# First attention of a two-layer kernel: the inner loop in half steps of two tiles instead of single tiles

## The chip, the cores and the metric

The kernel runs on one core of a Trainium2 chip. The metric is the device time of one execution in microseconds (us); lower is better. The engines are TensorE (PE, matrix products; PEld are its loads of weights), VectorE (DVE), ScalarE (ACT), GpSimd (POOL) and SyncE (SP, whose queue starts DMA transfers). Products land in PSUM, which has eight banks of 128 x 512 floats, and are read from there by VectorE or ScalarE.

## The reference

One sequence of 2048 tokens with 128 channels passes four stages. Each adds its result to x, and each works on a layer norm of x:

```python
x = x + L0_attn(layernorm(x))   # 16 heads of 64, low-rank q, k, v, rotary
x = x + L0_ffn(layernorm(x))    # 16 experts, 4 chosen per token in 2 of 4 groups
x = x + L1_attn(layernorm(x))   # 8 heads; 96 keys per query, chosen by an index score
x = x + L1_ffn(layernorm(x))    # shared expert and 2 of 8 experts by hash
```

The change is in the first stage. Its core, for each head, is

```python
scores = einsum('bhqd,bhkd->bhqk', q, k) * scale
attn = softmax(scores, axis=-1)          # over all 2048 keys
out = einsum('bhqk,bhkd->bhqd', attn, v)
out = out.reshape(b, s, H * DH) @ w_out.T + residual
```

All data are 32-bit floats.

## The kernel before, in words

The first attention has 32 units: eight pairs of heads times four groups of 512 queries, all pairs of a group before the next group. A unit has 16 tiles. The scores are computed twice, once with queries on the partitions and once with keys on the partitions.

*By query* (`by_query`, L313): for one tile of 128 queries and 512 keys, two products "pa" (L323), one for each head of the pair. Each uses 64 rows of TensorE's array, so that both run side by side (the form "64*128" in the profile's rows). VectorE then copies each, negated, into a tile "neg" and takes the smallest value of each row, which gives the largest score (L329). `sums` (L331) lets ScalarE take the exponential of the copy and add it up by row (L340). `close`, `inverse` and `turn` make of these the maximum and the sum of each query over all keys, and the row "mrow" with the maxima.

*By key* (`by_key`, L377): for one tile of 128 keys and 512 queries, two products "pb" (L384) of the same form, and two small bf16 products (L386) that subtract the maxima ("mrow"). ScalarE takes the exponential into a tile "e" (L390).

*Weighted block* (`mean`, L392): two products "po" (L399) that add the e-weighted latent values into one PSUM bank. They use 128 rows and 64 columns of the array each (form "128*64"). After the last tile of a unit, ScalarE copies the bank into "o" (L404), and `project` (L408) multiplies by the output weights and adds to x.

`rope` (L283) makes the rotated queries of the next unit and, for the first eight units, the rotated keys (L299, L302 on VectorE, the sum L303 on POOL); keys go out to DRAM and come back in pieces "ka" and "kb" by SP's queue, whose order is written by hand. Products of pa, pb and rope take turns in five PSUM banks (pool "ps"); "po" has one bank, and all other products share two (pool "px"). The tiles "e" and the two intermediate tiles of a rope share seven buffers.

`run` (L422) writes all this as steps of four tiles. By key runs five steps behind by query, and the weighted blocks one step behind by key. When the eight units of a group are done, the following three stages of that group (`follow`: `experts0`, `attention1`, `experts1`) are woven in: they are a generator, and `advance(us)` lets it issue as many of its pieces as the given time pays for. In `attention1`, `choose` (L820) searches the largest index scores on VectorE, `gather` fetches the chosen rows by DMAs that POOL issues, `queries` and `attend` do the rest; `rotate` (L92) is used for keys, queries and gathered keys. The stages of the fourth group run alone at the end.

Within an engine, instructions run in the order of the compiled program. A scheduler makes that order from the order of issue, from priorities (copies, sums and exponentials have a high one) and from its own estimate of when operands are ready.

Of the kernel before, what the change touches and what calls it, by code (L numbers as in the profile page):

```python
# [8 lines left out]
F32 = mybir.dt.float32  # L9
# [8 lines left out]
P = 128  # L18
T = 2048
NT = T // P  # L20
# [15 lines left out]

CHOSEN = [((11 * r) % NE1, (11 * r + 7919) % NE1) for r in range(8)]
NA = 2 * NT + 1
LATE = 1
URGENT = 500  # L40
PACE = (1.0, 1.1, 1.2, 1.2)

# [1 line left out]
def bcast(ap, axis, n):  # L44

    shape = list(ap.shape)
    return ap.unsqueeze(axis).to_broadcast(shape[:axis] + [n] + shape[axis:])
# [43 lines left out]

def rotate(nc, eng, pool, out1, out2, mu, cos, sin, tag, bufs=None, keep=None):  # L92

    shape = list(mu.shape)
    c = pool.tile(shape, F32, tag=tag + "c", name=tag + "c", bufs=bufs)
    s = pool.tile(shape, F32, tag=tag + "s", name=tag + "s", bufs=bufs)
    first = eng.tensor_tensor(c, mu, bcast(cos, 2, 2), ALU.mult)
    if keep is not None:
        keep(first)
    second = eng.tensor_tensor(s, mu, bcast(sin, 2, 2), ALU.mult)  # L100
    if keep is not None:
        keep(second)
    eng.tensor_tensor(out1, c[:, :, 0, :], s[:, :, 1, :], ALU.subtract)
    eng.tensor_tensor(out2, s[:, :, 0, :], c[:, :, 1, :], ALU.add)


class Program:
# [205 lines left out]
    def by_query(self, u, i):  # L313


        nc = self.nc
        kc, qt = divmod(i, 4)
        if i == 0:
            self.ms[u] = [self.am.tile([P, 4, 4, 2], F32, tag=f"mx{k}", name=f"mx{k}_{u}") for k in range(2)]
        q, k = self.qs[self.UNITS[u]], self.kcs[(u, kc, "a")]  # L320
        ps = [self.bank(f"pa{u}_{i}_{h}") for h in range(2)]
        for h, rows in enumerate(self.HALVES):
            nc.tensor.matmul(ps[h], q[rows, qt * P : qt * P + P], k[rows, :], start=True, stop=True)  # L323
        mx = self.ms[u][0]
        with self.tc.high_priority(URGENT):
            for h in range(2):
                at = (slice(None), qt, kc, slice(h, h + 1))
                t = self.negs[(u, i, h)] = self.am.tile([P, 512], F32, tag="neg", name=f"neg{u}_{i}_{h}", bufs=5)
                nc.vector.tensor_scalar(t, ps[h], -1.0, None, ALU.mult, ALU.min, accum_out=mx[at])  # L329

    def sums(self, u, i):  # L331
# [90 lines left out]
    def run(self):  # L422

        self.prologue()
        NU = len(self.UNITS)
        BEHIND = 5
        for c in range(2):  # L430
            self.keys_of(0, c, "a")
        stream, owed, pace = self.early, 0.0, 0.8

        def advance(us):
            nonlocal stream, owed
            if stream is None:
                return
            owed += us * pace
            while owed > 0 and stream is not None:
                cost = next(stream, None)  # L440
                if cost is None:
                    stream = None
                else:
                    owed -= cost


        with self.tc.manual_schedule(engines={mybir.EngineType.SP}):
            for s in range(4 * NU + BEHIND + 5):
                u, j = divmod(s, 4)
                ub, jb = divmod(s - BEHIND, 4)  # L450
                um, jm = divmod(s - BEHIND - 1, 4)
                if u < NU and j == 0 and u + 1 < NU:
                    self.rope(self.UNITS[u + 1][0], "q", self.UNITS[u + 1][1])
                if u + 1 < 8:
                    self.rope(u + 1, "k", j)
                if s == 4 * 8 - 4:
                    for _ in stream or ():
                        pass
                    stream, owed = None, 0.0
                    self.late.close()  # L460
                if s == 4 * 8:
                    self.keys.close()
                if s + 2 < 4 * NU:
                    self.keys_of((s + 2) // 4, (s + 2) % 4, "a")
                sb = s + 2 - BEHIND
                if 0 <= sb < 4 * NU:
                    self.keys_of(sb // 4, sb % 4, "b")
                for i in range(4):
                    if 0 <= ub < NU:
                        self.by_key(ub, 4 * jb + i)  # L470
                    advance(1.0)
                    if u < NU:
                        self.by_query(u, 4 * j + i)
                    advance(1.0)
                    n = 4 * s + i
                    if 0 <= n - LATE < 16 * NU:
                        self.sums(*divmod(n - LATE, 16))
                    if i == 3 and u < NU and j == 3:
                        self.close(u)
                    if i == 2 and j == 0 and 0 <= u - 1 < NU:  # L480
                        self.turn(u - 1)
                        self.inverse(u - 1)
                    if 0 <= um < NU:
                        self.mean(um, 4 * jm + i)
                    advance(1.0)
                    if i % 2 == 1 and jm == 1 and 0 <= um - 1 < NU:
                        self.project(um - 1, i // 2)
                if jm == 1 and 0 <= um - 1 < NU:
                    self.outs.pop(um - 1)
                    if um % 8 == 0:  # L490
                        if stream is not None:
                            for _ in stream:
                                pass
                        stream, owed = None, 0.0
                        if um < NU:
                            stream, pace = self.follow(um // 8 - 1), PACE[um // 8 - 1]

        self.first.close()
        self.alone = True
        for _ in self.follow(3):  # L500
            pass
# [219 lines left out]
    def attention1(self, sc, g):  # L721
# [4 lines left out]
        xr, cs, kT, kiT, table = self.xr[g], self.cs, self.kT, self.kiT, self.table  # L726
# [7 lines left out]
        with ExitStack() as prep:  # L734
# [17 lines left out]
            for i, (dst, wt) in enumerate(  # L752
# [5 lines left out]
                o, s = dst, pm[:m, :]  # L758
                if i in (1, 2):
                    o = o.rearrange("p (n a g) -> p n a g", a=4, g=32)  # L760
                    s = s.rearrange("p (n g a) -> p n a g", a=4, g=32)
# [17 lines left out]
        sm = sc.enter_context(tc.tile_pool(name="c_sm", bufs=2, side="right"))  # L779
# [8 lines left out]
        def index_scores(n):  # L788

            width = 64 + 128 * n  # L790
            q = slice(P * (n % 4), P * (n % 4) + P)
            v = sm.tile([P, T - 64], F32, tag="v", name=f"v{n}", bufs=2 if self.alone else 1)
            for lo in range(0, width, 512):
                hi = min(lo + 512, width)
                for h in range(4):
                    rows = slice(64 * (h % 2), 64 * (h % 2) + 64)
                    pi = self.x(f"pi{n}_{lo}_{h}", [P, 512])
                    nc.tensor.matmul(pi[:, : hi - lo], qiT[h // 2][rows, q], kiT[rows, lo:hi], start=True, stop=True)  # L798
                    if h == 0:
                        nc.vector.tensor_scalar(v[:, lo:hi], pi[:, : hi - lo], 0.0, w["iw"][:, 0:1], ALU.max, ALU.mult)  # L800
                    else:
                        rl = sm.tile([P, 512], F32, tag="rl", name=f"rl{n}_{lo}_{h}", bufs=6 if self.alone else 2)
                        nc.scalar.activation(rl[:, : hi - lo], pi[:, : hi - lo], AF.Relu)  # L803
                        nc.vector.scalar_tensor_tensor(  # L804
                            v[:, lo:hi], rl[:, : hi - lo], w["iw"][:, h : h + 1], v[:, lo:hi], ALU.mult, ALU.add
                        )
                    if h % 2 == 1:
                        yield pay(2.0)


            vmask = w["vmask"]
            if n == 0:
                nc.vector.tensor_tensor(v[:, 0:64], v[:, 0:64], vmask[:, 1, 0:64], ALU.min)
                nc.vector.tensor_copy(v[:, 64:128], vmask[:, 1, 64:128])
                width = P
            else:
                nc.vector.tensor_tensor(v[:, width - P : width], v[:, width - P : width], vmask[:, 0, :], ALU.min)
            vs[n] = v[:, 0:width]
# [83 lines left out]
        def attend(n):  # L902
            (kv, cl), (qs, ql) = chosen.pop(n), qTs.pop(n)

            for i in range(2):
                half = kv[:, 16 * i : 16 * i + 16, 32:64]

                rotate(
                    nc, nc.vector, sm, half[:, :, 0:16], half[:, :, 16:32],
                    half.rearrange("p r (a b) -> p r a b", a=2),  # L910
                    bcast(cs[:, 0, 2 * NT, :], 1, 16), bcast(cs[:, 1, 2 * NT, :], 1, 16), "rg", 1,
                    tc.keep_in_program_order,
                )
                yield pay(2.0)
# [317 lines left out]
```

## Time and profile before

| what | value |
|---|---|
| time, median of 5 runs | 3233.21 us |
| lowest and highest of the 5 | 3225.97 and 3250.67 us |
| the profiled execution's own time | 3255.46 us |
| its span, first to last instruction | 3253.4 us |
| mean granted clock of TensorE | 0.884 |
| waits of POOL's L303 for VectorE's t_q | 1028.4 us |
| waits of VectorE's L329 for TensorE's pa | 525.0 us |
| waits of ScalarE's L340 for VectorE's neg | 443.1 us |

A row of the profile's groups reads: line, engine, operation, output from input, shapes, count, then busy time in us and mean ns of one, then the idle time of that engine just before these instructions and what ended it. A row of a timeline reads: start in us from the span's start, duration in us, engine, line, operation, names, shapes, and how many instructions are merged. One product of 32-bit floats leaves two records, one for each of its two passes through the array. The slices show the span in 40 equal parts of 81 us, each digit the busy share in tenths.

### The profile page before, as it was taken

To read this page: it belongs to the slowest core of one execution; us is meant where nothing else is said; L and a number is where in the kernel's file an instruction comes from. 1 tells how busy PE (TensorE), PEld (TensorE's weight loads), DVE (VectorE), ACT (ScalarE), POOL (GpSimd) and SP (SyncE) were. 2 spreads that over 40 slices of the span, in tenths; PEclk is the share of its full clock that TensorE was granted. 3 is DMA by queue.
4 is the path that set the end of the run, shared out by engine and by line. 5 is a ranking of instruction groups with operands and counts; after the bars stand their busy time and mean duration, and the time that the engine had idled before them with its cause. 6 is when DMAs were issued, how large, how long until landed. Compare 5 with 4: busy or idle time off the path is not lost. (4 is left out here: it accounts for less than half of the span.)

```text
span 3253.4 us, 39029 instructions
## 1 busy us (share of the span) xinstructions
PE 2732.4 (84%) x13452; PEld 1136.1 (35%) x13452; DVE 1682.8 (52%) x4650; ACT 1801.0 (55%) x4190; POOL 580.9 (18%) x586
## 2 busy tenths in 40 slices
PE   6999999998798899997798889999789769773436
PEld 3333333343243344332233334343233324431224
DVE  7655554655344445664445534666526343585433
ACT  4777778666475567665465557656455435331224
POOL 2111000002313210002313220001222230007330
PEclk9999999999798899998798889999889789875557
DMA  4221111111111111111111111111111010101000
GB/s 147 60 59 49 59 49 41 49 42 37 33 34 40 32 46 48 41 41 30 34 31 38 30 27 54 46 46 27 30 30 35 22 24 27 40 14 25 13 13 28
DMA packets 98100, 127.76 MB, mean 39 GB/s; under 512 B 31344, under 2 KB 49776, under 8 KB 97904
## 3 DMA queue, kind: packets, MB, share of 16 engines
q1 hardware_dynamic: 81520, 108.48, 11.5%
q0 software_dynamic: 16384, 16.81, 2.2%
q8 instruction: 106, 1.74, 0.2%
q14 instruction: 90, 0.74, 0.1%
HBM read 115.26 MB, written 9.96 MB: 38 GB/s over the span
## 5 line engine op out<-in xcount | busy, mean ns | idle before, releaser
L329 DVE TENSOR_SCALAR_CACHE_REDUCE neg<-pa 128x512 f32<-128x512 f32 x1024 | 671.3, 686 | 680.5 <-PE pa L323 525.0
L340 ACT ACTIVATE neg<-neg,mx 128x512 f32<-128x512 f32 x1024 | 734.7, 718 | 497.4 <-DVE neg L329 443.1
L390 ACT ACTIVATE e<-pb 128x512 f32<-128x512 f32 x1024 | 554.6, 593 | 332.4 <-PE pb L386 234.0
L323 PE MATMUL pa<-ka,q 64*128 64x512 f32 x2048 | 677.8, 630 | 57.7 <-DVE neg L329 36.2
L384 PE MATMUL pb<-q,kb 64*128 64x512 f32 x2048 | 670.6, 661 | 58.7 <-ACT e L390 44.4
L843 POOL DMA_INDIRECT kv<-table,ixT x512 | 493.1, 963 | 804.8 <-issue 307.0
L399 PE MATMUL po<-e,ckv 128*64 128x512 f32 x2048 | 588.0, 640 | 9.5 <-issue 6.8
L323 PEld LDWEIGHTS pa<-ka,q 64*128 64x128 f32 x2048 | 239.7, 194 | 287.5 <-issue 105.2
L384 PEld LDWEIGHTS pb<-q,kb 64*128 64x128 f32 x2048 | 194.6, 192 | 404.0 <-DVE neg L329 145.0
L303 POOL TENSOR_TENSOR q<-t_q 128x512 f32<-128x512 f32 x32 | 40.9, 1278 | 1501.1 <-DVE t_q L302 1028.4
L386 PE MATMUL pb<-mrow,onesb 64*128 64x512 bf16 x1024 | 236.8, 388 | 4.0 <-issue 4.0
L399 PEld LDWEIGHTS po<-e,ckv 128*64 128x64 f32 x2048 | 106.6, 137 | 332.3 <-issue 301.9
L340 ACT ACTIVATION_READ_ACCUMULATOR neg<-neg,mx 128x1 f32 x1024 | 193.8, 189 | 0.0
L798 PE MATMUL pi<-kiT,qiT 64*128 64x512 f32 (+4 forms) x320 | 124.3, 659 | 56.9 <-issue 21.4
L951 DVE TENSOR_REDUCE mx<-pl 128x2 f32<-128x416 f32 x64 | 37.8, 591 | 245.4 <-remote 144.5
L955 ACT ACTIVATE e<-pl,mx 128x208 f32<-128x208 f32 x128 | 54.5, 431 | 172.1 <-DVE mx L952 155.2
L804 DVE SCALAR_TENSOR_TENSOR v<-rl,iw_sb,v 128x512 f32<-128x512 f32 (+4 forms) x120 | 77.2, 649 | 80.2 <-ACT rl L803 52.4
L945 PE MATMUL pl<-kr,qT 64*32 64x128 f32 x1024 | 61.6, 302 | 62.4 <-issue 62.4
L717 DVE SCALAR_TENSOR_TENSOR hb<-thb,zb 128x512 f32<-128x512 f32 x64 | 44.3, 692 | 127.3 <-ACT zb L715 127.3
L386 PEld LDWEIGHTS <-onesb 64*128 64x128 bf16 x1024 | 63.2, 97 | 124.1 <-issue 118.4
L803 ACT ACTIVATE rl<-pi 128x512 f32<-128x512 f32 (+4 forms) x120 | 57.5, 508 | 83.5 <-PE pi L798 36.2
L894 PE MATMUL ptq<-ident,qq 128*128 128x128 f32 x256 | 51.5, 344 | 61.8 <-issue 29.5
(276 smaller groups left out, 2871.0 us busy)
## 6 DMA issues: line engine op xcount, KB each, us to landing
ka<-kd SPq DMA_DIRECT2D x128, 256.0 KB
kb<-kd SPq DMA_DIRECT2D x128, 256.0 KB
wb<-in_wx SPq DMA_DIRECT2D x64, 192.0 KB
kd<-kst SPq DMA_DIRECT2D x32, 256.0 KB
kv<-table,ixT POOLq DMA_INDIRECT x512
wd<-in_wx SPq DMA_DIRECT2D x40, 192.0 KB
csk<-in_cs SPq DMA_DIRECT2D x4, 512.0 KB
csq<-in_cs SPq DMA_DIRECT2D x4, 512.0 KB
```

Source lines behind the costliest of these rows:

```text
L323: nc.tensor.matmul(ps[h], q[rows, qt * P : qt * P + P], k[rows, :], start=True, stop=True)
L329: nc.vector.tensor_scalar(t, ps[h], -1.0, None, ALU.mult, ALU.min, accum_out=mx[at])
L340: nc.scalar.activation(t, t, AF.Exp, bias=mx[at], scale=-1.0, accum_out=su[at])
L384: nc.tensor.matmul(ps[h], k[rows, c], q[rows, :], start=True, stop=False)
L386: nc.tensor.matmul(ps[h], self.onesb[rows, :], mrow[rows, :], start=False, stop=True)
L390: nc.scalar.activation(e[:, h, :], ps[h], AF.Exp)
L399: nc.tensor.matmul(self.pos[u][cols, :], self.ckv[:, kb, :], e[:, h, :], start=(kb == 0), stop=(kb == NT - 1))
L798: nc.tensor.matmul(pi[:, : hi - lo], qiT[h // 2][rows, q], kiT[rows, lo:hi], start=True, stop=True)
L803: nc.scalar.activation(rl[:, : hi - lo], pi[:, : hi - lo], AF.Relu)
L804: nc.vector.scalar_tensor_tensor(v[:, lo:hi], rl[:, : hi - lo], w["iw"][:, h : h + 1], v[:, lo:hi], ALU.mult, ALU.add)
L843: nc.gpsimd.indirect_dma_start(out=kv[:, 2 * (g % 16) + g // 16, :], out_offset=None, in_=table[0 : P * (n + 1), :], in_offset=bass.Indire ...
L945: nc.tensor.matmul(pl[32 * j : 32 * j + 32, c, 80:NK], qs[rows, 32 * gr : 32 * gr + 32], kr[rows, gr % 16, :], start=False, stop=(c == 1),)
```

## The change

Each step of four tiles is written as two halves of two tiles: two tiles by key, the sums of two earlier tiles, two tiles by query, two weighted blocks. Before, each tile had one of each in turn. The sums on ScalarE are issued two tiles behind their copies instead of one (`LATE`), and the copies "neg" get eight buffers instead of five. The following stages are given the same total of time in a step: one after each tile by key and by query, and two after the two weighted blocks.

Two more edits make space for the buffers. `rotate` puts its two intermediate tiles into one, and for the gathered keys of `attention1` takes the two buffers of the existing tag "w4", which `queries` and `attend` use too. The index scores "v" are allocated only as wide as the group needs.

```diff
...
-LATE = 1
+LATE = 2
...
-    shape = list(mu.shape)
-    c = pool.tile(shape, F32, tag=tag + "c", name=tag + "c", bufs=bufs)
-    s = pool.tile(shape, F32, tag=tag + "s", name=tag + "s", bufs=bufs)
+    a = mu.shape[1]
+    both = pool.tile([P, 64 * a], F32, tag=tag, name=tag, bufs=bufs).rearrange("p (k a b d) -> p k a b d", k=2, a=a, b=2)
+    c, s = both[:, 0], both[:, 1]
...
-                t = self.negs[(u, i, h)] = self.am.tile([P, 512], F32, tag="neg", name=f"neg{u}_{i}_{h}", bufs=5)
+                t = self.negs[(u, i, h)] = self.am.tile([P, 512], F32, tag="neg", name=f"neg{u}_{i}_{h}", bufs=8)
...
-                for i in range(4):
-                    if 0 <= ub < NU:
-                        self.by_key(ub, 4 * jb + i)
-                    advance(1.0)
-                    if u < NU:
-                        self.by_query(u, 4 * j + i)
-                    advance(1.0)
-                    n = 4 * s + i
-                    if 0 <= n - LATE < 16 * NU:
-                        self.sums(*divmod(n - LATE, 16))
-                    if i == 3 and u < NU and j == 3:
+                for half in range(2):
+                    pair = range(2 * half, 2 * half + 2)
+                    for i in pair:
+                        if 0 <= ub < NU:
+                            self.by_key(ub, 4 * jb + i)
+                        advance(1.0)
+                    for i in pair:
+                        n = 4 * s + i - LATE
+                        if 0 <= n < 16 * NU:
+                            self.sums(*divmod(n, 16))
+                    for i in pair:
+                        if u < NU:
+                            self.by_query(u, 4 * j + i)
+                        advance(1.0)
+                    if half == 1 and u < NU and j == 3:
                         self.close(u)
-                    if i == 2 and j == 0 and 0 <= u - 1 < NU:
+                    if half == 1 and j == 0 and 0 <= u - 1 < NU:
                         self.turn(u - 1)
                         self.inverse(u - 1)
-                    if 0 <= um < NU:
-                        self.mean(um, 4 * jm + i)
-                    advance(1.0)
-                    if i % 2 == 1 and jm == 1 and 0 <= um - 1 < NU:
-                        self.project(um - 1, i // 2)
+                    for i in pair:
+                        if 0 <= um < NU:
+                            self.mean(um, 4 * jm + i)
+                    advance(2.0)
+                    if jm == 1 and 0 <= um - 1 < NU:
+                        self.project(um - 1, half)
...
-            v = sm.tile([P, T - 64], F32, tag="v", name=f"v{n}", bufs=2 if self.alone else 1)
+            v = sm.tile([P, 512 * g + 448], F32, tag="v", name=f"v{n}", bufs=2 if self.alone else 1)
...
-                    bcast(cs[:, 0, 2 * NT, :], 1, 16), bcast(cs[:, 1, 2 * NT, :], 1, 16), "rg", 1,
+                    bcast(cs[:, 0, 2 * NT, :], 1, 16), bcast(cs[:, 1, 2 * NT, :], 1, 16), "w4", None,
...
```

## The prediction

> **What bounds the kernel now.** I read the page first: which engine is full, and where in the span.
>
> ```profile
> PE 2732.4 (84%) x13452; PEld 1136.1 (35%) x13452; DVE 1682.8 (52%) x4650; ACT 1801.0 (55%) x4190; POOL 580.9 (18%) x586
> PE   6999999998798899997798889999789769773436
> PEclk9999999999798899998798889999889789875557
> ```
>
> TensorE is nearly full from slice 2 to slice 34, about 90 to 2790 us: the first attention, alone at first and later beside the stream of the following stages. The last 460 us (the follow-up of the last group) are outside the change. Then the table by stretch, in columns stretch, PE, PEld, DVE, ACT, POOL, clock, DMA:
>
> ```profile
> 100.00:600.00 500.00, 499.38 (x2297) 178.26 (x2293) 260.39 (x810) 376.03 (x878) 39.52 (x31) 1.00 0.18 51
> 1200.00:1500.00 300.00, 292.23 (x1339) 118.44 (x1337) 175.53 (x549) 192.98 (x425) 5.08 (x4) 0.99 0.16 46
> 1500.00:1900.00 400.00, 321.00 (x1644) 127.83 (x1640) 186.16 (x493) 209.38 (x513) 125.92 (x130) 0.86 0.13 33
> ```
>
> Without a stream, and beside experts0, TensorE has no gap and the full clock. Beside attention1 (third row) it is 80% busy at 0.86: other queues hold it up. The same table for pb (L384) alone gives the tiles (four records each): 141 in 100 to 600; 171 in the other full stretches (600-800, 1200-1500, 1900-2200, 2400-2500); 199 beside attention1. Last, TensorE's timeline, since a full engine gains only by shorter work:
>
> ```profile
> 205.95 1.13 PE L299 MATMUL ps_k<-ckd,wuk_sb 64*128 64x512 f32 x4
> 206.91 1.02 PE L384 MATMUL pb<-q,kb 64*128 64x512 f32 x4
> 207.77 0.38 PE L386 MATMUL pb<-mrow,onesb 64*128 64x512 bf16 x2
> 207.99 1.02 PE L323 MATMUL pa<-ka,q 64*128 64x512 f32 x4
> 208.94 1.08 PE L399 MATMUL po<-e,ckv 128*64 128x512 f32 x4
> 209.95 1.13 PE L384 MATMUL pb<-q,kb 64*128 64x512 f32 x4
> 210.91 0.38 PE L386 MATMUL pb<-mrow,onesb 64*128 64x512 bf16 x2
> ```
>
> From start to start, pb takes 0.86 us behind ps_k, which has the same form of array (64*128), but 0.96 behind po (128*64). The change of form costs 0.10. And po behind po:
>
> ```profile
> 2783.55 1.93 PE L399 MATMUL po<-e,ckv 128*64 128x512 f32 x6
> 2785.41 1.12 PE L1083 MATMUL pyd<-hd,wd 128*128 128x512 f32 x2
> ```
>
> Six records in 1.86 us, start to start, against 1.01 for four: the inner passes run at 0.43, the last takes about 0.53 and the second 0.48, as behind any change of form.
>
> **The change, part by part.** *Pairs on TensorE.* Before, two tiles are twice pb 0.96, mrow 0.22, pa 0.95, po 1.01: 6.28 us. After: pb 0.96, mrow 0.22, pb 0.86, mrow 0.22, pa 0.86 (followed by its own form), pa 0.95, po 0.91 (0.48 + 0.43), po 0.96 (0.43 + 0.53): 5.94. A pair saves 0.34 us where nothing stands inside it. The compiled order says how often that is: changes between 64*128 and 128*64 fall from 761 to 339, 422 fewer of the 512 that 256 unbroken pairs would drop. The 70 pairs of 100 to 600 stand unbroken (140), which leaves 282 of 372, or 0.76, for the rest. Priced by stretch: 70 x 0.34 = 24 us; 85 pairs in the other full stretches x 0.34 x 0.76 = 22; 100 pairs beside attention1, 26 at most. There the saving can all be waited away, or all count; I take a third, 9, since TensorE is 80% busy but in one queue with the waits. Sum 55.
>
> *Banks.* "ps" has five, taken in turn, two per pb and two per pa. In the compiled order an allocation waits for the one five before it. Who empties them, from the rows by form and the timeline:
>
> ```profile
> L340 ACT ACTIVATE neg<-neg,mx 128x512 f32<-128x512 f32 x1024 | 734.7, 718 | 497.4 <-DVE neg L329 443.1 <-issue 18.8 <-DVE kv L104 9.0
> L329 DVE TENSOR_SCALAR_CACHE_REDUCE neg<-pa 128x512 f32<-128x512 f32 x1024 | 671.3, 686 | 680.5 <-PE pa L323 525.0 <-remote 77.8 <-PE pb L386 30.7
> ```
>
> ```profile
> 1632.78 1.09 ACT L390 ACTIVATE e<-pb 128x512 f32<-128x512 f32 x2
> 1633.64 0.69 DVE L329 TENSOR_SCALAR_CACHE_REDUCE neg<-pa 128x512 f32<-128x512 f32 x1 [1.83 <-PE pa L323]
> 1634.38 0.72 ACT L340 ACTIVATE neg<-neg,mx 128x512 f32<-128x512 f32 x1 [0.51 <-DVE neg L329]
> ```
>
> Worked through for a half step with pb at 0: the first pb is complete at 1.37 (0.41 after its mrow starts, with the hand-over), ScalarE empties the four pb banks by 3.55 (4 x 0.545), VectorE the four pa banks from 3.34 to 5.89 (0.62 each from start to start), and the four sums (0.72) run from 4.08 to 7.06. The next pb completes at 5.94 + 1.37 = 7.31. So ScalarE has 0.25 us to spare, and the tightest bank, the last pa's, is empty at 3.0 for a need at 3.11. Before, the pb of a tile waited for an e with 1.2 us to spare, for VectorE with 1.3; after, it is about 0.2 and 2.1. Without a stream it just fits. The copies o and mrow (0.57 each, once per unit) cost what exceeds 0.25, some of which the next rope's 0.86 takes back: 2 us in all. Where ropes of q and k come together (eight times) four more banks are taken, and one pb waits 0.4 us: 3 us.
>
> *Sums two tiles later (LATE 2, neg from 5 buffers to 8).* In the compiled order the four sums still stand directly behind the e's of their own half step, ahead of the next e's: priority places them as soon as VectorE is done. I count nothing, gain or loss, and VectorE's wait for a neg buffer can only fall.
>
> *Work ahead of means.* mean still follows by_key by four tiles; the seven "e" tiles hold, and e_14 of each unit waits for the rope's sum on POOL (L303), as before, with the same gathers queued ahead of it. The order of SP's loads and stores and of POOL's sums and gathers is the same, entry by entry, in both compiled programs. No change.
>
> *Space.* v is cut to its need. rotate's tiles join in one, and for the gathered keys take the two "w4" tiles. In the last two blocks of the tail, VectorE's L97 then waits for TensorE's transposes of qq: it started at 3168.79 while the sixteen transposes (0.21 each from 3168.26) ran until about 3172. The two rotations behind it move by about 1.5 us, and ptr on TensorE and everything later in the block with them: 2 blocks, 3 us, between 0 (ScalarE's copies decide) and 6.
>
> Sum: -55 + 2 + 3 + 3 = -47 us on the profiled execution's 3255.5: 3208. That execution was 22 us above the median, so 3186.
>
> [...] Pairs give four banks in a row to one engine, then four to the other. [...]
>
> **Rivals.** *A: TensorE's saving counts only without a stream.* 24 - 8 = 16 us, 3217. For it: 199 tiles run at about 80%, with waits for VectorE and POOL. Against: the 171 tiles beside experts0 run at 96% or more.
>
> *B: ScalarE comes too late (slower).* The tight bank is freed by ScalarE, in whose queue the stream's copies stand. A copy of 0.59 in each of the 185 half steps beside the stream, less 0.25, is 63 us of waits. In choose, VectorE gets up to six searches between two pairs of negs where three stood (1.42 each at 1216 columns): 4.3 us more per half step, about 24 times, 0 to 103 us. Together 3249 to 3352 against the forecast's 3186; with a quarter of the searches, 3275. It decides from 47 / 185 = 0.25 us of new waiting per half step. Against it: the stream brings TensorE work as well, which gives ScalarE time.
>
> *C: the passes do not get shorter* (po behind po needs new weights for each block): 3233 + 8 = 3241. The six po in a row speak against it.
>
> **How the numbers follow.** Forecast 0.55, A 0.22, C 0.06, B 0.17. No change means within 0.5%, 16 us, about what a measurement here can tell: 3217 to 3249. The forecast is all faster; A lies on the edge (0.13 faster, 0.09 same); C is same; B is slower but for 0.01. Faster 0.68, same 0.16, slower 0.16. The range: full price for the pairs beside attention1 and no costs gives 3233 - 72 = 3161, and the wider margin for VectorE may take a little more idle time: 3150. Upward it takes in A, C and the first part of B: 3260. Outside are the rest of B (0.1) and a larger gain (0.1).
>
> **What would show it.** Timeline without a stream: pb, pb, pa, pa, po, po in 5.94 us a pair, pb behind mrow in 0.86, po behind po in 0.43 a pass. Right: 100 to 600 holds about 149 tiles in place of 141, and PE's busy time falls by 50 to 70 us. A: idle time of TensorE before pa and pb grows by as much as busy time falls. B: waits "PE pa <- ACT e" of over 40 us, or a longer attention1 stretch. Wrong altogether if the pair takes 6.28 us.

## The result, and the profile after

The changed kernel takes 3228.8 us (median of 52 runs, 3216.6 to 3239.5) against 3233.8 us of the kernel before beside it (94 runs). The ratio is 0.998, 95% interval 0.9967 to 0.9993. The forecast was 3186: of the 47 us that it expected, 5 came. In the experiments below, where all times are shorter, the same kernel came out at 1.0027 (1.0016 to 1.0038) of the kernel before.

From the page of the changed kernel's profile:

```profile
span 3235.2 us, 38832 instructions
...
PE 2706.5 (84%) x13452; PEld 1225.3 (38%) x13452; DVE 1675.6 (52%) x4650; ACT 1787.7 (55%) x4190; POOL 583.8 (18%) x586
PE   6999999998797899997698879999769787874446
PEclk9999999998797799998898889999879797985656
```

TensorE's busy time fell by 26 us, not by 50 to 70. The stretches shown before, in columns stretch, PE, PEld, DVE, ACT, POOL, clock, DMA:

```profile
100.00:600.00 500.00, 496.49 (x2353) 208.59 (x2353) 271.31 (x848) 378.94 (x907) 39.19 (x31) 1.00 0.19 54
1200.00:1500.00 300.00, 287.19 (x1330) 127.19 (x1331) 177.33 (x551) 192.76 (x423) 6.96 (x6) 0.98 0.15 44
1500.00:1900.00 400.00, 317.70 (x1632) 138.69 (x1630) 184.85 (x489) 206.99 (x510) 117.47 (x124) 0.86 0.12 32
```

Without a stream TensorE is still full (496.49 us busy of 500). From 1200 to 1500 us it now has 13 us of pauses where it had 8, at a clock of 0.98 where it had 0.99. TensorE's timeline without a stream shows the pair:

```profile
208.01 1.13 PE L384 MATMUL pb<-q,kb 64*128 64x512 f32 x4
208.97 0.38 PE L386 MATMUL pb<-mrow,onesb 64*128 64x512 bf16 x2
209.19 1.02 PE L384 MATMUL pb<-q,kb 64*128 64x512 f32 x4
210.05 0.38 PE L386 MATMUL pb<-mrow,onesb 64*128 64x512 bf16 x2
210.26 1.97 PE L323 MATMUL pa<-ka,q 64*128 64x512 f32 x8
212.16 1.94 PE L399 MATMUL po<-e,ckv 128*64 128x512 f32 x8
214.03 1.13 PE L299 MATMUL ps_k<-ckd,wuk_sb 64*128 64x512 f32 x4
```

pb 0.96, mrow 0.22, pb 0.86, mrow 0.21, pa 1.90, po 1.87: 6.02 us from start to start, for 5.94 forecast. The groups by form say what the banks do over the whole span. First pa and pb of the kernel before:

```profile
L323 PE MATMUL pa<-ka,q 64*128 64x512 f32 x2048 | 677.8, 630 | 57.7 <-DVE neg L329 36.2 <-issue 11.1 <-DVE t_q L302 6.3
L384 PE MATMUL pb<-q,kb 64*128 64x512 f32 x2048 | 670.6, 661 | 58.7 <-ACT e L390 44.4 <-issue 9.8 <-DVE neg L329 3.6
```

Then the changed kernel:

```profile
L340 ACT ACTIVATE neg<-neg,mx 128x512 f32<-128x512 f32 x1024 | 729.6, 714 | 390.0 <-DVE neg L329 362.3 <-DVE w L97 12.8 <-issue 7.2
L329 DVE TENSOR_SCALAR_CACHE_REDUCE neg<-pa 128x512 f32<-128x512 f32 x1024 | 658.6, 686 | 616.6 <-PE pa L323 444.2 <-remote 139.7 <-ACT e L390 8.4
L323 PE MATMUL pa<-ka,q 64*128 64x512 f32 x2048 | 649.8, 650 | 127.7 <-ACT e L390 71.6 <-issue 44.6 <-DVE w L97 6.1
L384 PE MATMUL pb<-q,kb 64*128 64x512 f32 x2048 | 684.3, 646 | 43.5 <-DVE neg L329 23.5 <-issue 8.3 <-DVE t_q L302 7.6
```

VectorE waits less for TensorE's pa (444.2 us where it was 525.0), and ScalarE's sums less for VectorE's neg (362.3, was 443.1). TensorE waits more: 127.7 us before pa where it was 57.7, and 71.6 of it for ScalarE's e. Before pb it waits less, 43.5 us where it was 58.7, so the two together grew by 55 us.

Where it went, read at the copies o that end each unit: the end of unit 8 moved from 618.4 to 598.1 us (20 us won), units 9 to 31 beside the stream grew from 2174.5 to 2206.9 (32 lost), and the tail behind them fell from 460.5 to 430.3. The last number did not come back: in the experiments the tail is 349 to 358 us in all kernels, 356.8 for the old order with the new space and 352.4 for the changed kernel. I take the 30 us for chance of the two executions. Without it the two profiles would give +12 us where the medians give -5, so some of the 32 will be chance too; one execution of each cannot say how much.

### The profile page after: what moved, and what is told of

It reads as the page before. It is cut to its first block, busy times and chain, and to the rows that moved or that the text cites. A ratio compares the mean times of both kernels' runs of the same rounds, so it can differ in the third digit from the quotient of the medians.

```text
span 3235.2 us, 38832 instructions
## 1 busy us (share of the span) xinstructions
PE 2706.5 (84%) x13452; PEld 1225.3 (38%) x13452; DVE 1675.6 (52%) x4650; ACT 1787.7 (55%) x4190; POOL 583.8 (18%) x586
## 5 line engine op out<-in xcount | busy, mean ns | idle before, releaser
L329 DVE TENSOR_SCALAR_CACHE_REDUCE neg<-pa 128x512 f32<-128x512 f32 x1024 | 658.6, 686 | 616.6 <-PE pa L323 444.2
L340 ACT ACTIVATE neg<-neg,mx 128x512 f32<-128x512 f32 x1024 | 729.6, 714 | 390.0 <-DVE neg L329 362.3
L323 PE MATMUL pa<-ka,q 64*128 64x512 f32 x2048 | 649.8, 650 | 127.7 <-ACT e L390 71.6
L384 PE MATMUL pb<-q,kb 64*128 64x512 f32 x2048 | 684.3, 646 | 43.5 <-DVE neg L329 23.5
L399 PE MATMUL po<-e,ckv 128*64 128x512 f32 x2048 | 538.2, 635 | 4.9 <-issue 4.9
L323 PEld LDWEIGHTS pa<-ka,q 64*128 64x128 f32 x2048 | 256.8, 197 | 361.2 <-ACT e L390 157.9
L384 PEld LDWEIGHTS pb<-q,kb 64*128 64x128 f32 x2048 | 231.6, 193 | 290.8 <-issue 142.6
L386 PE MATMUL pb<-mrow,onesb 64*128 64x512 bf16 x1024 | 263.2, 392 | 11.4 <-issue 5.8
L399 PEld LDWEIGHTS po<-e,ckv 128*64 128x64 f32 x2048 | 131.5, 142 | 321.7 <-issue 304.7
L340 ACT ACTIVATION_READ_ACCUMULATOR neg<-neg,mx 128x1 f32 x1024 | 192.0, 188 | 0.0
L386 PEld LDWEIGHTS <-onesb 64*128 64x128 bf16 x1024 | 71.2, 97 | 134.3 <-issue 124.7
L418 DVE SCALAR_TENSOR_TENSOR xr<-pp,rs,xr 128x128 f32<-128x128 f32 x256 | 72.1, 342 | 42.5 <-PE pp L415 42.5
L808 ACT ACTIVATE rl<-pi 128x512 f32<-128x512 f32 (+4 forms) x120 | 57.0, 508 | 58.7 <-PE pi L803 31.7
```

Source lines behind the costliest of these rows:

```text
L340: nc.scalar.activation(t, t, AF.Exp, bias=mx[at], scale=-1.0, accum_out=su[at])
L384: nc.tensor.matmul(ps[h], k[rows, c], q[rows, :], start=True, stop=False)
L386: nc.tensor.matmul(ps[h], self.onesb[rows, :], mrow[rows, :], start=False, stop=True)
L399: nc.tensor.matmul(self.pos[u][cols, :], self.ckv[:, kb, :], e[:, h, :], start=(kb == 0), stop=(kb == NT - 1))
L418: nc.vector.scalar_tensor_tensor(xr[:, j, :], pm[:, j, :], self.rs[u][:, j, h : h + 1], xr[:, j, :], ALU.mult, ALU.add)
```

## The experiments

Theory 1 was the forecast's own sum with rival B beside the stream: pairs save on TensorE everywhere, and there wait for ScalarE. All ratios are against the kernel before on the same chip, where it takes 2837 to 2841 us; what is known of the distance to 3234 stands at the end. The experiments ran on three chips: e1 to e4 on one, e5 to e12 on another, e13 to e16 on the third. "Stream" is the work of the following stages. "Units 9 to 31" runs from the copy o of unit 8 to that of unit 31.

**Which part of the change counts: e1, e2, e5.** e1 has the old loop and `LATE = 1` in the changed kernel; e2 has the new loop and `LATE = 2` in the kernel before; e5 is the changed kernel.

> The order of before, tile by tile with the sums one tile later, but with the changed kernel's space: rotate's joined tiles, the gathered keys' in the two w4 tiles, v cut to its need, eight neg buffers. Theory 1 (the pairs save 0.34 us each on TensorE and lose it again beside the stream, where the fifth bank of a pair waits for ScalarE; the shorter tail of the changed kernel's profile is chance): no change, 3230 to 3238 us, tail 460 us from the last copy of o. Theory 2 (the space edits shorten the tail by 20 to 30 us and the pairs alone bring nothing or lose): 3203 to 3215 us, tail 430 us.

> The half steps of two tiles and the sums two tiles later, with the space of before (rotate, v, five neg buffers). Theory 1: all of the change is in the order, so 3224 to 3234 us as the changed kernel. Theory 2: the order alone loses what the space edits hid, 3245 to 3260 us.

> The changed kernel itself, beside the kernel before on one chip with the others. Theory 1 (20 us won up to unit 8, 25 to 35 us lost in units 9 to 31, the space and the eight neg buffers nothing): 1.000 to 1.004 of the kernel before where the two stretches are as in the run of the half steps alone. Theory 2 (space edits and neg buffers shorten the tail): 0.990 to 0.995.

Measured: e1 0.9998 (0.9987 to 1.001), e2 1.0027 (1.0016 to 1.0038), e5 1.0027 (1.0016 to 1.0038). Space and buffers are worth nothing; the order of the loop is the whole effect. Up to unit 8 e5 wins 19 us over e1 (599.1 against 618.2), in units 9 to 31 it loses 29 (1889.8 against 1861.3), in the tail it wins 4. e2, on e1's chip, gives the same picture: 599.7, 1890.6 and a tail of 351.5. The table by stretch of e1, then of e5, for units 9 to 31:

```profile
618.20:2479.60 1861.40, 1778.35 (x9450) 734.38 (x9450) 1084.85 (x3074) 1227.07 (x2880) 397.29 (x404) 0.99 0.17 42
```

```profile
599.10:2489.00 1889.90, 1780.18 (x9448) 801.95 (x9448) 1081.48 (x3074) 1225.45 (x2882) 395.07 (x404) 0.97 0.15 42
```

The same matmuls take the same busy time, although each pair saves 0.27 us without a stream. The clock column suggests the reason: 0.97 in place of 0.99.

**Pairs in part: e3, e4.** e3 keeps the half steps where `stream is None` and runs the old loop otherwise. e4 pairs only the weighted blocks:

```diff
                     for i in pair:
                         if 0 <= ub < NU:
                             self.by_key(ub, 4 * jb + i)
                         advance(1.0)
+                        if u < NU:
+                            self.by_query(u, 4 * j + i)
+                        advance(1.0)
...
```

> The changed kernel, with half steps only where no stream runs beside them (some 72 of 256 pairs), and single tiles in the order of before where one does. Theory 1: the gain without a stream stays (20 us up to the end of unit 8) and the loss beside it goes: 3208 to 3218 us; units 9 to 31 take 2174 us as before. Theory 2: the same and the tail's 20 to 30 us: 3183 to 3195. A third theory, that the gain of the first units is always given back later because something else sets the end of the first attention: 3228 to 3234.

> The changed kernel with pb, pa, pb, pa, po, po in a half step in place of pb, pb, pa, pa, po, po: pb and pa have the same form of array, so the po's alone are paired and a pair still takes 5.94 to 6.02 us of TensorE without a stream, but ScalarE and VectorE empty banks in turn, two each. Theory 1 (banks held by ScalarE): the waits of PE pa for ACT e fall from 72 us to under 30, and the time to 3195 to 3213 us. If the loss beside the stream comes from elsewhere (the two po in a row, the stream's place, stalls by chance): 3225 to 3235, with units 9 to 31 at 2200 us or more.

Measured: e3 0.994 (0.9926 to 0.9955), with units 9 to 31 at 1860.8 us, as tile by tile. So the gain of the first units is not taken back by anything later; the loss arises beside the stream. e4 0.9942 (0.9921 to 0.9963): the same gain without a stream (601.9 us at the end of unit 8) and 1869.1 us beside it, in an execution 6 us longer than its median. As theory 1 had it, the waits of pa for e go; but waits for VectorE's neg come in their place. The waits, as engine, line, what was waited for, us, times, longest, of e5 and then of e4 (PEld is the load of weights, PE the product itself):

```profile
PEld pa L323 <- ACT e L390: 101.3, 284, 3.6
PE pa L323 <- ACT e L390: 17.0, 20, 2.7
PE pa L323 <- DVE neg L329: 8.3, 2, 6.1
```

```profile
PEld pa L323 <- ACT e L390: 4.4, 22, 0.3
PE pa L323 <- DVE neg L329: 51.0, 32, 6.5
```

**Does ScalarE come too late: e6, e7, e9.** e6 and e7 shorten the sums L340 in the kernel before and in the changed one; e9 ties each sum behind the e's that the program issued ahead of it:

```diff
-                nc.scalar.activation(t, t, AF.Exp, bias=mx[at], scale=-1.0, accum_out=su[at])
+                a = nc.scalar.activation(t, t, AF.Exp, bias=mx[at], scale=-1.0, accum_out=su[at])
+                if self.last_e is not None:
+                    self.tc.add_manual_dep(
+                        a.ins, self.last_e.ins.name,
+                        mybir.DependencyInfo(mybir.DependencyClass.NoSync, mybir.DependencyReason.DATA),
+                        reason="behind",
+                    )
```

> The kernel before with the sums L340 over 128 of the 512 columns (they leave out three quarters of each sum, and the sum is kept above 0.01 so that its reciprocal stays finite): ScalarE has some 1.4 us less to do per two tiles. ScalarE does not bound the order tile by tile, so both theories expect little: 0.985 to 1.0 of the kernel before. It is the base for the next one.

> The changed kernel with the same short sums. Theory 1 (in half steps the banks wait for ScalarE): with 1.4 us more room the loss beside the stream goes, units 9 to 31 take 25 to 45 us less than those of the kernel before with short sums, and the whole is 40 to 60 us under it (ratio 0.980 to 0.986 of it). Rival (the stream's own matmuls stand inside the pairs and break them, or VectorE is late): units 9 to 31 stay 15 to 35 us longer than those of the kernel before with short sums.

> The changed kernel with each sum L340 tied in ScalarE's queue behind the e's of the half step in which the program issues it, so that ScalarE's order is four e's and then the four sums of the half step before. Theory 1 (in half steps the banks wait for ScalarE, whose e's stand behind sums that wait for VectorE's negs): ScalarE gets 0.88 us to spare in place of 0.25, the waits of PEld pa for ACT e fall from 101 us to under 40, units 9 to 31 from 1890 to between 1840 and 1865 us, and the ratio to the kernel before is 0.984 to 0.993. Rival (the loss comes from VectorE's four negs in a row, from pairs that the stream breaks, or from the lower clock alone): units 9 to 31 at 1880 us or more, ratio 1.000 or above.

Measured: e6 0.9902 (0.9881 to 0.9923), e7 0.9831 (0.981 to 0.9852). Units 9 to 31 take 1842.9 and 1845.3 us: with less work on ScalarE (189 us less busy time there in e6 than in e1, 178 less in e7 than in e5, about 1 us a pair where 1.4 was estimated) the loss of 29 shrinks to 2, but the saving does not appear. In all, e7 is 20 us under e6, where theory 1 expected 40 to 60. e9 1.0002 (0.9991 to 1.0013): the rival's number. The tie did to ScalarE what was expected. Its row in front of the four e's, without a stream, in e5 and then in e9:

```profile
211.15 2.10 ACT L390 ACTIVATE e<-pb 128x512 f32<-128x512 f32 x4 [0.39 <-PE pb L386]
```

```profile
208.08 2.10 ACT L397 ACTIVATE e<-pb 128x512 f32<-128x512 f32 x4 [1.12 <-PE pb L393]
```

ScalarE now waits 1.12 us for the pb, not 0.39, and units 1 to 4 take 55.0 us, not 55.5. Beside the stream it did not help (1898.3 us). The waits of e5 (those of pa stand above) and then of e9:

```profile
PE pi L803 <- ACT rl L808: 5.8, 6, 1.5
PE py L703 <- ACT zb L720: 3.9, 8, 0.9
```

```profile
PEld pa L324 <- ACT e L397: 66.9, 233, 3.6
PE pa L324 <- ACT e L397: 5.7, 6, 2.7
PE pi L810 <- ACT rl L815: 15.1, 12, 2.2
PE py L710 <- ACT zb L727: 15.1, 12, 1.3
```

The weight loads' wait for the e's fell by a third, and that of pa itself from 17.0 us to 5.7. Instead the stream's own matmuls pi and py, whose ScalarE work (rl, zb) stands in the same queue, waited 20 us longer.

**Both engines shorter: e11, e12.**

> The kernel before with negs L329 and sums L340 over 128 of their 512 columns (three quarters of the maxima and sums are left out; q is scaled by a thousandth so that the exponentials stay finite): VectorE and ScalarE both have some 1.4 us less per two tiles. It is the base for the next one: 0.975 to 0.992 of the kernel before.

> The changed kernel with the same short negs and sums. With short sums alone units 9 to 31 were 2 us longer than tile by tile, where shorter passes on TensorE promise 30 to 48 us less. Theory 1b (the rest is VectorE's four negs in a row): units 9 to 31 come out 20 to 45 us under those of the kernel before with short negs and sums. Theory 1c (the rest is the stream's own matmuls inside the pairs, its waits and the lower clock): within 8 us of them, as with short sums alone.

Measured: 0.9666 (0.9649 to 0.9683) and 0.9634 (0.9617 to 0.9651); units 9 to 31 take 1786.0 and 1795.8 us, 10 us more in half steps. Theory 1b is out, and 1c nearly holds. This clears VectorE's negs and ScalarE's sums, but not the emptying of pb's banks: the e's had their full length, and in e12 pa's weights waited for them nearly as long as in e5 (101.3 us):

```profile
PEld pa L323 <- ACT e L390: 95.6, 281, 3.7
```

**The clock.** In every trace here the granted clock of TensorE is either 1.0 or 0.5, and the spells of 0.5 last 3.41 us or a multiple of it, but for those cut off by the end of a trace (48 spells in the profile before, 57 in the one after). Counted from the traces for units 9 to 31, in us; "pauses" are stops of TensorE of 2 us and more, and the last column is the busy time less half of that part of it which fell in half clock:

| kernel | units 9 to 31 | idle | at half clock | pauses | busy, as at full clock |
|---|---|---|---|---|---|
| e1, tile by tile | 1861 | 83 | 44 | 4 | 1758 |
| e5, half steps | 1890 | 110 | 123 | 15 | 1722 |
| e9, half steps, sums tied | 1898 | 135 | 116 | 14 | 1711 |
| e11, e1's order, both short | 1786 | 47 | 27 | 3 | 1728 |
| e12, half steps, both short | 1796 | 66 | 68 | 8 | 1700 |
| before, first comparison | 2174 | 272 | 389 | 30 | 1784 |
| after, first comparison | 2207 | 313 | 457 | 38 | 1745 |

This is where the gain went. In half steps the passes need 36 us less at full clock (39 in the first comparison, 28 with both engines shorter). TensorE then idles 27 us more, and the time at half clock grows by 79 us, of which it works through 76; half of that is 38: -36 + 27 + 38 = 29. The three terms add up to the difference by how they are counted; what they tell is their sizes. Of the 27 us of idle time, 25 lie in pauses of 2 us and more (16.6 us in e1, 41.8 in e5), and of the 79 us at half clock 58 lie in spells that begin in such a pause or within 4.5 us of its end (23.9 us in e1, 81.9 in e5). The 15 pauses of e5 have no one owner: five end with VectorE's neg, three with ScalarE's e, the other seven with five other tiles of the attention and of the stream. In e5, 14 of the 15 are followed by half clock within 4.5 us of their end; of its 21 stops of 1 to 2 us, 6, and of its 84 stops of under 1 us, 8. One of the long pauses on TensorE's timeline of e5, with the table of the spell that follows:

```profile
1056.03 1.93 PE L323 MATMUL pa<-ka,q 64*128 64x512 f32 x6
1060.11 1.22 PE L323 MATMUL pa<-ka,q 64*128 64x512 f32 x2 [2.15 <-ACT e L390]
...
1062.74 2.75 PE L399 MATMUL po<-e,ckv 128*64 128x512 f32 x8
...
1071.38 1.94 PE L399 MATMUL po<-e,ckv 128*64 128x512 f32 x8
```

```profile
1061.01:1064.42 3.41, 3.41 (x13) 1.75 (x14) 0.70 (x2) 3.29 (x10) 0.69 (x1) 0.50 0.54 159
```

The last of a pair's four pa matmuls waits 2.15 us for the e that holds its bank; the two weighted blocks behind it then take 2.75 us in place of 1.94.

So far this goes together, no more. e4 shows that long pauses are not all: it has eight, and 102 us at half clock, of which 48 lie behind them. e13 and e14 make the pauses themselves, in units 1 to 7 of e1's order, which have none:

```diff
+                    held = ExitStack()
+                    if 4 <= s < 32 and (j, i) == (1, 0):
+                        held.enter_context(self.tc.issue_after(self.pause(4 * s + i, 5).ins))
...
+    def pause(self, n, reps):
...
+        pz = self.x(f"pz{n}")
...
+            self.tc.keep_in_program_order(nc.tensor.matmul(pz[:, 0, 0:32], self.ident, self.ident[:, 0:32], start=True, stop=True))
+            nc.vector.tensor_copy(self.z[:, 0:32], pz[:, 0, 0:32])
+            for _ in range(reps):
+                nc.vector.tensor_scalar(self.z, self.z, 1.0, None, ALU.mult)
+            return nc.tensor.matmul(pz[:, 1, 0:32], self.z[:, 0:128], self.ident[:, 0:32], start=True, stop=True)
```

e14 has `reps` 0 and four places, `(j, i) in ((1, 0), (2, 0), (2, 2), (3, 0))`.

> The order tile by tile with the changed kernel's space and five neg buffers; in units 1 to 7, which run without a stream, TensorE has to stop once per unit, for a tiny matmul that waits for six operations in a row on VectorE (2 to 4 us). Theory (a pause over 2 us halves the clock for 3.4 us or more): the clock of units 1 to 7 falls from 1.00 to about 0.97, seven spells of half clock in 390 us, and each unit takes its pause and 1.7 us or more on top. Rival (the half clock beside the stream has other causes): the clock stays at 1.00 and a unit takes its pause alone.

> The same with four pauses per unit, each for one short operation on VectorE (0.7 to 1.2 us), so that the idle time of a unit is about that of the one long pause. Theory: the clock stays at 0.99 to 1.00 and a unit takes its pauses alone. Rival (idle time counts, however it is spread): the same fall of the clock as with one long pause.

Measured, from one profiled execution each: in e13 six pauses of 2.6 to 4.5 us lie behind 150 us, and six of six are followed by half clock, for 3.4 or 6.8 us; the clock of units 1 to 8 is 0.976. In e14 the ten recorded stops of 1.1 to 1.2 us bring one spell, and the clock is 0.997. TensorE behind a long pause of e13, and behind a short one of e14:

```profile
290.81 0.41 PE L434 MATMUL pz<-ident,z 128*128 128x32 f32 x2 [4.46 <-DVE z L433]
291.14 2.04 PE L384 MATMUL pb<-q,kb 64*128 64x512 f32 x4
292.97 0.65 PE L386 MATMUL pb<-mrow,onesb 64*128 64x512 bf16 x2
293.39 1.65 PE L323 MATMUL pa<-ka,q 64*128 64x512 f32 x4
294.97 1.08 PE L399 MATMUL po<-e,ckv 128*64 128x512 f32 x4
```

```profile
284.75 0.41 PE L434 MATMUL pz<-ident,z 128*128 128x32 f32 x2 [1.13 <-DVE z L431]
285.09 1.13 PE L384 MATMUL pb<-q,kb 64*128 64x512 f32 x4
286.05 0.38 PE L386 MATMUL pb<-mrow,onesb 64*128 64x512 bf16 x2
286.27 1.02 PE L323 MATMUL pa<-ka,q 64*128 64x512 f32 x4
287.22 1.08 PE L399 MATMUL po<-e,ckv 128*64 128x512 f32 x4
```

pb, mrow and pa take 3.83 us behind the long pause and 2.13 behind the short one. So this long pause, followed by one spell of 3.41 us, costs 1.70 us on top of its own length; three of the six were followed by a spell of 6.83 us. e14 has less idle time than e13, 14.9 us in units 1 to 8 against 22.0, since only two of a unit's four pauses show at that length; but its half clock there is 3.4 us against 23.9. So pauses of 2.6 to 4.5 us brought half clock, six of six, and stops of 1.1 to 1.2 us did so once in ten, in one execution of each; what a pause between these lengths does, the two do not show. In e5, 11 of the 12 pauses of 2 to 3 us were followed by half clock.

**Coarse or fine: e8, e10, e15, e16.** e8 gives the stream all of its time at the end of a half step. e10 is e4's loop with e9's tie, e15 the kernel before with the tie, e16 the changed loop where no stream runs and e10's beside one.

> The changed kernel with all of the stream's work of a half step at its end (one advance of 6 in place of 1, 1, 1, 1 and 2), so that none of its matmuls stands inside a pair. Theory 1 (banks wait for ScalarE): no better, since the stream's ScalarE work now comes in one lump ahead of the next e's; ratio 1.000 to 1.010 of the kernel before. Rival (broken pairs lose the saving): units 9 to 31 take 30 us less than in the changed kernel, ratio 0.985 to 0.993.

> The order pb, pa, pb, pa, po, po with the sums tied behind the e's in the same way (two tiles late). Theory 1: a little better than that order without the tie, ratio 0.986 to 0.993, units 9 to 31 at 1845 to 1865 us. If that order's banks wait for VectorE alone (46 us of PE pa for DVE neg against 33 tile by tile): no better than without, 0.993 to 0.997.

> The kernel before (tile by tile, its own space, five neg buffers), with each sum tied behind the e's of the tile in which the program issues it, one tile late. If the tie alone brings what e10 showed: ratio 0.985 to 0.990. If the tie only lifts the limit that ScalarE sets in other orders: 0.997 to 1.003, since the order tile by tile does not wait for ScalarE.

> Half steps pb, pb, pa, pa, po, po where no stream runs, pb, pa, pb, pa, po, po beside one, sums tied behind the e's in both. Units 1 to 8 as in e9 (590 us at the end of unit 8), units 9 to 31 as in e10 (1858 us), tail 350: 2798 to 2806 us, ratio 0.985 to 0.988. If the two orders disturb each other where they meet: 0.990 or above.

Measured: e8 1.029 (1.0271 to 1.0309), above both expectations; the coarsest order, with units 9 to 31 at 1961.7 us, 20 pauses and 167 us at half clock. e10 0.9875 (0.9855 to 0.9894): 595.4 us at the end of unit 8, 1858.5 beside the stream. e15 1.003 (1.0015 to 1.0045): the tie alone brings nothing. e4's order without the tie brought 0.9942, so about half of e10's gain comes only with both. e16 0.9893 (0.9873 to 0.9913): 592.3 and 1854.7 as expected, but 2810 us in all and not 2798 to 2806; its tail was 358 us where e10's was 349. e10 and e16 are equal within their intervals, and both beat the kernel before and the changed one, by 1.1 to 1.5%. Beside the stream, though, they are only 3 and 7 us under e1 (1861.3): their gain lies mostly in the units without a stream, and no order here brought the 36 us of shorter passes home beside it.

## Why the prediction was wrong, and where it was right

- *Passes of TensorE: right, a little large.* A pair takes 6.02 us where 5.94 was forecast; a unit of eight pairs fell by 2.2 us, 0.27 a pair and not 0.34. Up to unit 8 that is 20 us for the 24 priced. From 100 to 600 us the trace has 144 tiles by pb's records, for 149 forecast and 141 before.
- *The failed step: the saving beside the stream, 22 for 85 pairs in full stretches and 9 for 100 beside attention1.* The passes did get shorter by about as much, 36 us at full clock against 31. But the stretch grew, by 29 us (32 in the first comparison). Split by unit in e5 against e1: the ten units that lie mostly in those full stretches of the profile before (9, 10, 15 to 18, 23 to 25, 28) lost 7.1 us where 22 were priced as gain, the others lost 21.4 where 9 were. In the first comparison's two profiles the same ten lost 13. So a full TensorE did not protect the saving. The reading behind it was a little high, too: the table before has a clock of 0.97 in 1900 to 2200 us and TensorE 95% busy in 2400 to 2500, where "full clock" and "96% or more" were read. "The saving can all be waited away, or all count; I take a third" left out a third case, that the pairs make the waits longer. And a wait was priced at its length; with the half clock behind it, the pause measured in e13 cost 1.7 us besides, and e5's 14 spells behind long pauses, 5.9 us each, up to 2.9.
- *Banks: margin right, consequence not.* 0.25 us to spare was worked out and 0.39 is seen without a stream. Beside it, pa's weight loads wait 101 us for e in e5 and 4.5 in the profile before, whose order e1 has, and pa itself 17 us in e5; the sum had 2 + 3 us for banks, both for work of the first attention, and nothing for the stream's. Rival B named this place, and its sign, over 40 us of pa waiting for e, came in the profile after (71.6 us). But lateness of ScalarE was only part: short sums took away 26 of 29 us of loss, and e9's tie none of it.
- *What remains is coarseness, argued from the row of experiments.* An engine taken for 2.1 us and then 2.8 in a row (half steps) would keep the stream's next step waiting longer than in parts of half that length. e8, e5, e4, e10 stand in this order at 1962, 1890, 1869 and 1859 us, with 118, 110, 101 and 90 us of idle time and 167, 123, 102 and 96 at half clock. The number of long pauses does not follow (20, 15, 8 and 12). And e8 does not fit the account whole: of its 72 us over e5, 44 are passes that are longer as at full clock (1766 against 1722), for which no cause was found. No single wait was isolated that carries it all.
- *LATE 2 and eight buffers: right as far as tested.* e2 and e5 are equal without and with the space and the buffers, and even real lateness (e9) brings 0.5 us a unit without a stream and nothing beside it. No run changed `LATE` alone.
- *Space: 3 us of loss expected in the tail, none found.* e1's tail is 356.8 us, as e15's is with the old space (356.8), and e1's ratio is 0.9998.
- *Rivals.* A (3217) was nearest in its first half, since only the units without a stream gained; it did not see the loss. B was right that the stretch beside the stream grows, but its price was 63 to 166 us over the forecast, and its cause, the stream's copies and searches, was not tested by itself. C is out: the passes are shorter.

## What to carry to other kernels

Saving passes on a full engine by doing two of each kind in a row also lengthens the time for which its partners are held (ScalarE by the e's: 1.09 us tile by tile, 2.10 in half steps); price that against the work that shares their queues, stage by stage. Count TensorE's pauses by length and not only their sum, since in e5 those of 2 us and more, 41.8 us in all, had 81.9 us at half clock behind them, about as much again in lost time. Where a coarse order gains alone and loses in company, pair only the step that pays (here po: e4 0.9942, e10 0.9875), and keep the engines that empty banks taking turns.

## What was not expected of the hardware

The granted clock in these traces has two values, 1.0 and 0.5, with spells of 0.5 in multiples of 3.41 us, and in units 9 to 31 of e5 against e1 the longer half clock cost 38 us where the waits cost 27.

The same program took two different times. The kernel before took 3234 us in the first comparison and 2837 to 2841 on the three chips of the experiments. Its unit 8 ended at 618.4 us in the first, and that of e1, its order, at 618.2: alone, the first attention runs alike. In the first comparison's execution TensorE, VectorE and ScalarE stand still together for over 1 us 82 times, 226 us in all, up to 33 us at once; in e1's 6 times, 12 us. Half clock in units 9 to 31 is 389 us there and 44 in e1. What stops all three was not found, nor whether it is the chip.
